# Cross-attention and a ternary feed-forward on one core: heads taken in pairs per batch, keys made on chip, score matmuls as 64-row tiles

## The chip, the cores and the metric

The kernel runs on one core of a Trainium2 chip. The metric is device time in microseconds (us) from the start to the end of one launch; lower is better. Three runs of the kernel before took 846.71, 849.12 and 853.64 us. Durations below come from one further execution that the hardware profiler recorded.

Engines: PE is the matrix engine (PEld its weight loads), DVE the vector engine, ACT the scalar engine, POOL the general engine, SP the engine that issues all the DMAs here. Each works through its own queue in order.

## The reference

`x` is [2, 512, 512] (batch, rows, width), the context `ctx` is [2, 1024, 128]. All of it is fp32.

```python
def layer(x, ctx):
    h = layernorm(x)
    q = (h @ Wq.T).reshape(2, 512, 16, 128)              # 16 heads
    q_big = rope(einsum('bshk,hkq->bshq', q, w_kc_q))    # 384 wide
    q_r = einsum('bshq,hqr->bhsr', q_big, W_qr)          # 64 wide
    kv_r = rope(ctx)                                     # [2, 1024, 128]
    k_r = einsum('bld,hdr->bhlr', kv_r, W_kr)            # 64 wide
    attn = softmax(einsum('bhsr,bhlr->bhsl', q_r, k_r))  # 512 x 1024 per head
    c = einsum('bhsl,bld->bhsd', attn, kv_r)
    x = x + heads(einsum('bhsd,hkd->bhsk', c, w_kc_kv)) @ Wo.T
    y = layernorm(x)                                     # feed-forward:
    return x + bit(silu(bit(y, gate)) * bit(y, val), out)
```

`bit` rounds activations to 8 bits per row and the weights to {-1, 0, 1} times their mean magnitude, then multiplies and adds a bias.

## The kernel before

**Precision.** A value that must be exact to fp32 is held as a high part (`_hi`, fp32r, rounded) and a low part (`_lo`, the rest); a product is three matmuls: high by high, high by low, low by high. The softmax weights are split the same way into two fp16 halves.

**A step** is one head of one batch: 32 steps, in the order of `STEPS`, a table written by hand (twelve heads in pairs, then a special order for the last four). For each step `q_down`, `q_up`, the rotary functions `rot_*` and `q_rank` make the 64-wide query of 512 rows, and `t_hi`, `t_res`, `t_lo` (L613 to L624) arrange it in two tiles `t1`, `t2` of 128 partitions: `t1` holds the high part twice, `t2` holds the low part and the rest.

**Keys.** `key_make` (L870) multiplies `kv_r` by the `W_kr` of two heads, for eight pairs of heads and four blocks of 512 columns: 32 calls of three matmuls, all of them in the first 104 us. `key_hi` and `key_lo` evict the bank. `key_store` (L883) writes both parts to DRAM in two DMAs (60 in all), and `load_keys` (L500) reads them back per step, in two DMAs of 256 KB (60 in all), so that a head's high part lies on partitions 0 to 63 and its low part on 64 to 127. The first two heads get theirs straight from SBUF (`key_direct`, 8 DMAs).

**Scores and softmax.** A step has four *strips* of 128 query rows by 1,024 keys. `score` (L627) makes a strip in four 128-row matmuls, two for each half of the columns:

```python
ps = sc[i, st] = psc.tile([P, L], F32, tag="sc", name=f"sc{i}_{st}")
for n, a in enumerate((t1, t2)):
    for c in range(2):
        nc.tensor.matmul(ps[:, cols], lhsT=a[:, rows], rhs=keys[i][:, cols], start=n == 0, stop=n == 1)
```

A strip then goes through `s_max` (DVE, L638), `s_exp` (ACT, L642, with a read of the sum), `s_scale` and `s_recip` (DVE, 128x1), `e_hi` (ACT, L654), `e_lo` (DVE, L659), and `e_turn` (L665), a transposing DMA that SP issues. `e_lo` is the last that reads the strip's PSUM tile. The pool `psc` has two such tiles, two banks each; the other four banks (`psb`) serve all the other matmuls. The pool `ep` has two tiles for the fp16 weights, which come free when `e_turn` has landed.

**After the softmax** `mix` (L667) multiplies the turned weights by `kv_r`; `c_hi`, `c_lo` evict a step's 512 columns at once; `project` (L684) and `accumulate` (L695) add two heads at a time to `x1`, through `wos[h]`, the product of `w_kc_kv` and `Wo` that `w_out` makes.

**Beside it**, from about 60 us on, the feed-forward weights are read twice: `load_sum`, `w_sum` for their mean magnitude, then `load_tern`, `w_round` (POOL), `w_clip` (DVE), `w_tern` (POOL), `w_store`, in 48 pieces of 512 columns. The feed-forward (`ff_*`) takes the last 100 us.

**The order of issue** is a table, `ISSUE`: for each function a list of places, made by a planner that is not in the file. Calls are sorted by place, and `keep_order` (L411) fixes each engine's order to that. Nothing is reordered at run time; an instruction that waits holds up all behind it on its engine.

Of the kernel before, what the change touches and what calls it, by code (L numbers as in the profile page):

```python
# [1 line left out]

# [23 lines left out]
P = 128  # L26
# [10 lines left out]
STEPS = [(2 * p + n, b) for p in range(6) for b in range(B) for n in range(2)]  # L37
STEPS += [(12, 0), (13, 0), (12, 1), (14, 0), (15, 0), (15, 1), (14, 1), (13, 1)]
NI = len(STEPS)

SPLITS = list(range(H)) + [13]
SPLIT = [h for h, _ in STEPS[:-1]] + [H]

# [3 lines left out]
        760, 701, 693, 742, 895, 812, 888, 941, 1101, 1204, 1135, 1086, 1245, 1192, 1327, 1223, 1507, 1458, 1483,  # L47
        1536, 1600, 1682, 1718, 1649, 1875, 1884, 1925, 1993, 2022, 2044, 2148, 2129, 2303, 2327, 2389, 2521, 2468,
        2532, 2480, 2608, 2674, 2725, 2688, 2809, 2838, 2963, 3027, 2913, 3040, 3110, 3130, 3180, 3396, 3346, 3436,
        3372, 3253, 3243, 3245, 3228, 3474, 3461, 3463, 3458,  # L50
    ),
    "b_hi": (221, 477, 602, 719, 917, 1219, 1350, 1449, 1798, 1974, 2201, 2354, 2578, 2799, 2914, 3124),
    "b_lo": (273, 502, 613, 801, 969, 1290, 1357, 1546, 1802, 1998, 2250, 2375, 2588, 2829, 2979, 3171),
    "c_hi": (
        525, 611, 688, 776, 856, 987, 1043, 1142, 1303, 1368, 1438, 1558, 1668, 1800, 1849, 1990, 2107, 2209, 2285,
        2409, 2536, 2621, 2696, 2803, 2887, 2989, 3075, 3159, 3212, 3292, 3365, 3439,
    ),
    "c_lo": (
        528, 621, 697, 779, 866, 1003, 1053, 1147, 1308, 1375, 1440, 1571, 1670, 1823, 1861, 2004, 2121, 2217, 2291,
        2417, 2549, 2625, 2704, 2804, 2895, 2997, 3084, 3183, 3219, 3300, 3373, 3440,  # L60
    ),
    "e_hi": (
        288, 306, 354, 381, 410, 446, 481, 508, 537, 558, 575, 616, 641, 662, 681, 694, 724, 743, 770, 790, 819, 837,
        854, 881, 901, 925, 943, 972, 989, 1011, 1029, 1059, 1080, 1108, 1129, 1149, 1189, 1212, 1240, 1248, 1291,
        1309, 1337, 1356, 1394, 1417, 1446, 1472, 1502, 1527, 1551, 1579, 1596, 1627, 1647, 1675, 1698, 1722, 1754,
        1777, 1790, 1839, 1844, 1895, 1899, 1937, 1945, 1982, 2007, 2035, 2058, 2088, 2106, 2127, 2158, 2191, 2203,
        2229, 2253, 2275, 2302, 2329, 2353, 2371, 2400, 2423, 2451, 2475, 2510, 2539, 2552, 2577, 2611, 2627, 2657,
        2680, 2697, 2732, 2752, 2773, 2805, 2824, 2847, 2875, 2893, 2909, 2949, 2955, 2987, 2996, 3038, 3023, 3083,
        3092, 3122, 3141, 3160, 3174, 3216, 3234, 3264, 3277, 3316, 3318, 3342, 3354, 3376, 3389,
    ),  # L70
    "e_lo": (
        296, 319, 359, 382, 423, 465, 486, 519, 539, 573, 577, 623, 645, 666, 684, 703, 744, 745, 774, 798, 827, 839,
        863, 885, 911, 927, 946, 973, 1000, 1019, 1041, 1065, 1087, 1117, 1146, 1162, 1194, 1215, 1250, 1258, 1292,
        1324, 1339, 1374, 1408, 1420, 1451, 1481, 1505, 1534, 1557, 1581, 1616, 1630, 1654, 1688, 1704, 1726, 1759,
        1778, 1795, 1846, 1854, 1897, 1907, 1954, 1958, 1986, 2015, 2036, 2068, 2091, 2111, 2133, 2167, 2194, 2214,
        2238, 2267, 2282, 2317, 2332, 2357, 2379, 2402, 2428, 2455, 2484, 2515, 2541, 2569, 2591, 2618, 2635, 2661,
        2683, 2708, 2733, 2757, 2782, 2810, 2827, 2861, 2885, 2901, 2916, 2952, 2957, 2990, 3000, 3041, 3028, 3088,
        3103, 3126, 3145, 3162, 3185, 3221, 3241, 3271, 3281, 3317, 3321, 3352, 3357, 3386, 3393,
    ),
    "e_turn": (  # L80
        309, 366, 403, 414, 453, 497, 518, 523, 545, 599, 607, 638, 648, 683, 707, 729, 766, 771, 791, 813, 831, 857,
        892, 898, 926, 959, 962, 992, 1006, 1046, 1068, 1092, 1095, 1137, 1167, 1179, 1202, 1226, 1267, 1281, 1306,
        1330, 1363, 1385, 1444, 1456, 1465, 1512, 1523, 1548, 1565, 1612, 1629, 1644, 1678, 1711, 1721, 1751, 1766,
        1810, 1814, 1859, 1888, 1909, 1927, 1959, 1972, 2014, 2024, 2063, 2104, 2126, 2152, 2159, 2176, 2215, 2237,
        2256, 2273, 2311, 2351, 2359, 2387, 2401, 2432, 2467, 2476, 2504, 2523, 2568, 2598, 2605, 2649, 2651, 2666,
        2717, 2735, 2768, 2783, 2802, 2812, 2836, 2870, 2888, 2917, 2931, 2967, 2978, 2999, 3020, 3073, 3079, 3101,
        3127, 3144, 3166, 3195, 3201, 3231, 3260, 3286, 3289, 3332, 3334, 3359, 3371, 3404, 3407,
    ),
    "ff_end": (3673, 3641, 3766, 3719, 3813, 3812, 3816, 3821),
    "ff_gate": (  # L90
        3401, 3408, 3424, 3417, 3455, 3482, 3485, 3457, 3525, 3539, 3503, 3497, 3562, 3577, 3548, 3582, 3604, 3625,
        3634, 3611, 3668, 3674, 3652, 3642, 3693, 3725, 3688, 3715, 3754, 3767, 3772, 3745,
    ),
    "ff_hint": (
        3462, 3501, 3490, 3472, 3554, 3570, 3559, 3567, 3608, 3635, 3628, 3614, 3643, 3646, 3665, 3660, 3697, 3722,
        3703, 3709, 3741, 3768, 3747, 3753, 3770, 3782, 3788, 3778, 3801, 3804, 3803, 3802,
    ),
    "ff_hmax": (
        3418, 3435, 3445, 3438, 3469, 3498, 3505, 3489, 3563, 3568, 3593, 3585, 3596, 3620, 3617, 3623, 3645, 3658,
        3654, 3657, 3692, 3696, 3702, 3704, 3729, 3748, 3731, 3749, 3779, 3787, 3791, 3784,  # L100
    ),
    "ff_hround": (
        3451, 3460, 3475, 3450, 3541, 3522, 3553, 3556, 3603, 3615, 3619, 3599, 3631, 3638, 3651, 3653, 3695, 3710,
        3691, 3700, 3728, 3738, 3737, 3736, 3755, 3760, 3761, 3758, 3794, 3796, 3799, 3798,
    ),
    "ff_hscale": (3448, 3518, 3598, 3626, 3679, 3716, 3751, 3793),
    "ff_hturn": (3531, 3590, 3636, 3676, 3733, 3775, 3792, 3807, 3811),
    "ff_in": (
        3392, 3394, 3395, 3400, 3410, 3421, 3405, 3406, 3446, 3449, 3468, 3484, 3479, 3491, 3444, 3447, 3514, 3515,
        3523, 3529, 3496, 3504, 3494, 3502, 3545, 3546, 3564, 3566, 3536, 3537, 3572, 3578, 3583, 3589, 3607, 3616,  # L110
        3618, 3627, 3592, 3594, 3659, 3661, 3663, 3672, 3644, 3648, 3632, 3640, 3685, 3690, 3714, 3718, 3677, 3680,
        3699, 3711, 3744, 3746, 3756, 3763, 3764, 3765, 3724, 3732,
    ),
    "ff_int": (3377, 3398, 3399, 3442, 3573, 3601, 3586, 3705),
    "ff_max": (3362, 3341, 3355, 3339, 3550, 3542, 3551, 3544),
    "ff_norm": (3356, 3326, 3347, 3325, 3535, 3524, 3534, 3530),
    "ff_out": (
        3533, 3547, 3560, 3579, 3595, 3600, 3624, 3629, 3656, 3675, 3723, 3742, 3682, 3708, 3713, 3717, 3743, 3774,
        3781, 3785, 3786, 3790, 3795, 3800, 3805, 3806, 3808, 3809, 3810, 3818, 3819, 3820,
    ),  # L120
    "ff_prod": (
        3416, 3420, 3441, 3429, 3467, 3495, 3500, 3477, 3540, 3555, 3538, 3521, 3575, 3587, 3569, 3602, 3609, 3639,
        3650, 3633, 3683, 3686, 3669, 3666, 3721, 3739, 3706, 3734, 3769, 3783, 3789, 3762,
    ),
    "ff_residual": (3397, 3344, 3415, 3343, 3740, 3797, 3664, 3687),
    "ff_round": (3368, 3391, 3390, 3411, 3565, 3591, 3574, 3597),
    "ff_scales": (3364, 3558),
    "ff_silu": (
        3413, 3414, 3427, 3419, 3464, 3483, 3487, 3471, 3528, 3549, 3519, 3509, 3571, 3580, 3552, 3584, 3606, 3630,
        3647, 3613, 3670, 3684, 3667, 3662, 3701, 3730, 3698, 3720, 3757, 3776, 3780, 3752,  # L130
    ),
    "ff_store": (3727, 3681, 3777, 3735, 3814, 3815, 3817, 3822),
    "ff_turn": (3387, 3432, 3433, 3532, 3581, 3621, 3610, 3707),
    "ff_value": (
        3402, 3409, 3434, 3423, 3453, 3488, 3492, 3452, 3527, 3543, 3516, 3511, 3561, 3576, 3557, 3588, 3605, 3622,
        3637, 3612, 3671, 3678, 3655, 3649, 3694, 3726, 3689, 3712, 3759, 3771, 3773, 3750,
    ),
    "hid_norm": (18, 30, 15, 25, 189, 147, 149, 192),
    "hid_part": (28, 38, 44, 58, 23, 33, 45, 53, 199, 209, 162, 169, 173, 177, 211, 216),
    "hid_turn": (19, 34, 17, 29, 194, 152, 154, 208),  # L140
    "key_direct": (123, 119, 157, 159),
    "key_hi": (
        59, 49, 62, 357, 294, 268, 218, 424, 129, 89, 223, 174, 431, 263, 339, 342, 161, 295, 146, 472, 275, 375, 244,
        459, 187, 180, 467, 251, 330, 361, 207, 387,
    ),
    "key_lo": (
# [278 lines left out]
def cross_attention_ffn(ctx: ExitStack, tc, x, ctxt, wall, wkr, tq, tk, fw, fbias, out):  # L425
# [67 lines left out]
    def key_direct(i, q):  # L493
        if q == 0:
            keys[i] = kst.tile([P, L], F32R, tag="ks", name=f"ks{i}")
# [704 lines left out]
```

## Time and profile before

| | |
|---|---|
| three runs, median (range) | 849.12 us (846.71 to 853.64) |
| the profiled execution, its time | 849.62 us |
| its span, first to last instruction | 847.8 us |
| first score matmul starts | 59.7 us |
| last strip's `s_max` starts | 740.7 us |
| end of the span after it | 107.1 us |
| bytes moved by DMA | 169.93 MB |
| granted clock of PE, mean | 0.955 |

In the page's rows a group is a line of the code on one engine: its count, its busy time in us, the mean duration in ns of one, and the idle time of the engine just ahead of it with what ended that. Two instructions of a group that overlap count once in busy time. The table of slices cuts the span in 40 equal parts; each digit is the busy share of a part in tenths.

### The profile page before, as it was taken

What the parts mean: (1) busy time and instruction counts of PE and PEld (TensorE: products, weight loads), DVE (VectorE), ACT (ScalarE), POOL (GpSimd) and SP (SyncE); (2) the same over time, 40 slices, a digit from 0 to 9 for tenths busy, and PEclk for the clock granted to TensorE, in tenths of its full rate; (3) what the DMA queues carried; (4) which work ended last, traced back from release to release, by engine and by line L of the source; (5) the groups of instructions that cost most, each with busy time, mean ns of one, the idle gap of its engine ahead of it and who ended that gap; (6) DMA issues with size and microseconds to landing.
All of it is one profiled execution on the core that took longest, in us unless ns stands there. A gap on an engine that the chain in (4) does not pass through costs nothing. (4 is left out here: it accounts for less than half of the span.)

```text
span 847.8 us, 12448 instructions
## 1 busy us (share of the span) xinstructions
PE 756.7 (89%) x3914; PEld 548.0 (65%) x3923; DVE 707.6 (83%) x1155; ACT 648.2 (76%) x1090; POOL 589.3 (70%) x529
## 2 busy tenths in 40 slices
PE   6699989989798988678989898898999998899997
PEld 4477756767686766456657676676877776554443
DVE  7899867879778888676879798787999797889995
ACT  4589978889787877666868787677888787859863
POOL 5488876675667777655768788877986694166773
PEclk7699999999999999899989999999999999999999
DMA  9679999998979999986989999979989999954345
GB/s 284 224 255 288 281 224 242 178 211 175 204 165 226 214 238 226 210 183 136 227 194 232 195 198 197 206 157 216 222 159 179 265 173 255 235 107 136 69 99 130
DMA packets 332976, 169.93 MB, mean 200 GB/s; under 512 B 292848, under 2 KB 298992, under 8 KB 332144
## 3 DMA queue, kind: packets, MB, share of 16 engines
q1 hardware_dynamic: 332912, 169.16, 88.5%
q8 instruction: 31, 0.51, 0.2%
q14 instruction: 33, 0.27, 0.1%
HBM read 71.60 MB, written 24.12 MB: 113 GB/s over the span
## 5 line engine op out<-in xcount | busy, mean ns | idle before, releaser
L674 PE MATMUL mps<-et,kvh 128*128 128x256 f16 x1024 | 184.3, 281 | 17.9 <-DMA et<-e 11.8
L659 DVE SCALAR_TENSOR_TENSOR e<-sc,m,e 128x1024 f16<-128x1024 f32 x128 | 163.1, 1279 | 32.2 <-ACT e L654 30.3
L638 DVE TENSOR_REDUCE m<-sc 128x1 f32<-128x1024 f32 x128 | 155.6, 1217 | 32.1 <-PE sc L634 30.6
L654 ACT ACTIVATE e<-sc,m 128x1024 f16<-128x1024 f32 x128 | 142.2, 1114 | 52.2 <-DMA et<-e 39.9
L634 PE MATMUL sc<-ks,t 128*128 128x512 f32 x512 | 148.0, 411 | 21.8 <-DVE e L659 11.9
L642 ACT ACTIVATE sc<-sc,m 128x1024 f32<-128x1024 f32 x128 | 139.5, 1090 | 22.6 <-DVE m L638 22.0
L593 POOL TENSOR_TENSOR c<-c,sinq 128x512 f32<-128x512 f32 x96 | 123.1, 1285 | 44.3 <-ACT c L580 29.6
L604 POOL TENSOR_TENSOR l<-u,h 128x512 fp32r<-128x512 f32 x96 | 123.4, 1290 | 34.5 <-ACT h L600 34.2
L674 PE MATMUL mps<-et,kvl 128*128 128x256 f16 x512 | 143.1, 280 | 0.0
L596 POOL TENSOR_TENSOR u<-u,c 128x512 f32<-128x512 f32 x96 | 124.4, 1299 | 21.2 <-DVE u L590 10.1
L674 PEld LDWEIGHTS <-kvh 128*128 128x128 f16 x1024 | 91.1, 101 | 70.0 <-issue 39.3
L634 PEld LDWEIGHTS sc<-ks,t 128*128 128x128 f32 x512 | 91.4, 191 | 51.0 <-issue 19.9
L590 DVE TENSOR_TENSOR u<-ups,cosq 128x512 f32<-128x512 f32 x96 | 65.2, 682 | 6.9 <-POOL l L604 3.6
L557 PE MATMUL qps<-hidh,whi 128*128 128x512 f32 x128 | 56.6, 443 | 8.8 <-DVE x L697 6.6
L1001 PE MATMUL gv<-ffw,fqt 128*128 128x512 bf16 x250 | 58.8, 379 | 3.7 <-DVE g L1009 2.1
L600 ACT CAST h<-u 128x512 fp32r<-128x512 f32 x96 | 59.0, 618 | 3.0 <-POOL u L596 2.9
L730 POOL TENSOR_SCALAR ft<-ft,fgw 128x512 f32<-128x512 f32 x48 | 33.5, 697 | 38.5 <-DMA ft<-in_fg 14.0
L737 POOL TENSOR_SCALAR fo<-ft 128x512 bf16<-128x512 f32 x48 | 29.7, 618 | 41.9 <-DVE ft L733 24.4
L692 PE MATMUL pps<-woh,ch 128*128 128x512 f32 x128 | 52.5, 410 | 5.7 <-ACT c L580 3.1
L674 PEld LDWEIGHTS <-kvl 128*128 128x128 f16 x512 | 51.4, 100 | 7.0
L557 PE MATMUL qps<-hidl,whi 128*128 128x512 f32 x128 | 53.4, 417 | 0.0
L557 PE MATMUL qps<-hidh,wlo 128*128 128x512 f32 x128 | 52.8, 412 | 0.0
(156 smaller groups left out, 1651.0 us busy)
## 6 DMA issues: line engine op xcount, KB each, us to landing
ks<-kd SPq DMA_DIRECT2D x60, 256.0 KB, 4.6
rawa<-in_wall SPq DMA_DIRECT2D x17, 544.0 KB, 4.8
kd<-kh SPq DMA_DIRECT2D x30, 256.0 KB, 2.9
kd<-kl SPq DMA_DIRECT2D x30, 256.0 KB, 3.2
fd<-fo SPq DMA_DIRECT2D x48, 128.0 KB, 3.0
rawb<-in_wall SPq DMA_DIRECT2D x16, 320.0 KB, 4.3
fs<-in_fg SPq DMA_DIRECT2D x16, 256.0 KB, 3.4
ft<-in_fg SPq DMA_DIRECT2D x16, 256.0 KB, 3.5
```

Of the source, the lines that this page charges most:

```text
L557: nc.tensor.matmul(qs[i][0], lhsT=a[:, c * K:(c + 1) * K], rhs=m[b][:, c, :], start=c == 0 and n == 0, stop=c == 3 and n == 2,)
L590: nc.vector.tensor_tensor(us[i, j], up[i, j], cosq[:, j, :], ALU.mult)
L593: nc.gpsimd.tensor_tensor(cs[i, j], cs[i, j], sinq[:, j, :], ALU.mult)
L596: nc.gpsimd.tensor_tensor(us[i, j], us[i, j], cs.pop((i, j)), ALU.add)
L600: nc.scalar.copy(hs[i, j], us[i, j])
L604: nc.gpsimd.tensor_tensor(ls[i, j], us.pop((i, j)), sb(hs[i, j]), ALU.subtract)
L634: nc.tensor.matmul(ps[:, cols], lhsT=a[:, rows], rhs=keys[i][:, cols], start=n == 0, stop=n == 1)
L638: nc.vector.tensor_reduce(m[:, 0:1], sc[i, st], AX.X, ALU.max, negate=True)
L642: nc.scalar.activation(ps, ps, AF.Exp, bias=m[:, 0:1], accum_out=m[:, 1:2])
L654: nc.scalar.activation(e[:, 0, :], sc[i, st], AF.Copy, scale=sm[i, st][:, 2:3])
L659: nc.vector.scalar_tensor_tensor(e[:, 1, :], sc.pop((i, st)), m[:, 2:3], e[:, 0, :], ALU.mult, ALU.subtract)
L674: nc.tensor.matmul(ps, lhsT=a[:, b, c, :], rhs=et[:, m + c, :], start=c == 0 and n == 0, stop=c == 7 and n == 2)
```

## The change

**Units.** A unit is a pair of heads of one batch, 16 in all, in plain order: `UNITS = [(p, b) for p in range(8) for b in range(B)]`. The special last order and the second read of head 13's weights go.

**Keys when due.** The DRAM copy of the keys is gone, with `key_store`, `load_keys` and `key_direct`: 128 DMAs. The rotated context stays in SBUF (`kth`, `ktl`), `W_kr` comes in eight small loads (`load_wk`), and each unit makes its own keys: two blocks, three matmuls, `key_hi`, `key_lo`, in all as many as before. Head 0 of the pair lies on partitions 0 to 63, head 1 on 64 to 127.

**Scores of two heads.** `t1`, `t2` and the keys hold the two heads of a unit on the two halves of the partitions. `score(u, st)` takes both tiles of `psc` and issues twelve matmuls of 64 rows, alternating between the heads: for each half of the columns high by high, high by low, low by high. `t_hi` becomes one eviction per head instead of two; the rest goes through a scratch tile of the pool `cp`.

**Smaller pieces.** `mix` has a bank per 256 columns, and `c_hi`, `c_lo` run per 256 columns (64 calls of each instead of 32). `wop` has 2 buffers of each kind instead of 4, `lp` 2 instead of 3. In the feed-forward, tiles come from other pools. Each call takes its tile when it runs, and `follow` adds an order (no wait) between users of a tag on different engines.

**A new `ISSUE`.** Every list of places is new. With it, all eight loads of `x` are issued ahead of nearly all the rest, and the first weights of `load_a` come after the tables and most of the context.

The core of the diff:

```diff
+UNITS = [(p, b) for p in range(8) for b in range(B)]
+STEPS = [(2 * p + e, b) for p, b in UNITS for e in range(2)]
...
-    def load_keys(i):
-        h, b = STEPS[i]
-        r = (h % 2) * 64
-        cols = slice(b * L, (b + 1) * L)
-        k = keys[i] = kst.tile([P, L], F32R, tag="ks", name=f"ks{i}")
-        nc.sync.dma_start(sb(k[0:64, :]), kd[h // 2][r:r + 64, 0, cols])
-        nc.sync.dma_start(sb(k[64:128, :]), kd[h // 2][r:r + 64, 1, cols])
+    def load_wk(p):
+        wkp[p] = [const.tile([P, 2 * R], F32, tag="wkr", name=f"wkr{p}")]
+        nc.sync.dma_start(wkp[p][0], wkr[:, p * 2 * R:(p + 1) * 2 * R])
...
+    def t_hi(i):
+        u, e = divmod(i, 2)
+        if u not in ts:
+            ts[u] = [t1p.tile([P, S], F32R, tag="t1", name=f"t1_{u}")]
+        nc.scalar.copy(ts[u][0][half(e), :], rs[i][half(e), :])
+
     def t_res(i):
-        t1, t2 = ts[i]
-        nc.vector.tensor_tensor(t2[64:128, :], rs[i][0:64, :], sb(t1[0:64, :]), ALU.subtract)
+        u, e = divmod(i, 2)
+        td[i] = late["cp"].tile([P, S], F32, tag="c", name=f"d{i}")
+        nc.vector.tensor_tensor(td[i][half(1 - e), :], rs[i][half(e), :], sb(ts[u][0][half(e), :]), ALU.subtract)
...
+    def key_make(u, c):
+        p, b = UNITS[u]
+        kps[u, c] = bank(f"kps{u}_{c}")
+        for n, (a, k) in enumerate(((0, kth), (0, ktl), (1, kth))):
+            nc.tensor.matmul(kps[u, c], lhsT=wkp[p][1][:, a, :], rhs=k[b][:, block(c)], start=n == 0, stop=n == 2)
...
+    def score(u, st):
         rows = slice(st * P, (st + 1) * P)
-        ps = sc[i, st] = psc.tile([P, L], F32, tag="sc", name=f"sc{i}_{st}")
-        for n, a in enumerate((t1, t2)):
-            for c in range(2):
-                cols = slice(c * 512, (c + 1) * 512)
-                nc.tensor.matmul(ps[:, cols], lhsT=a[:, rows], rhs=keys[i][:, cols], start=n == 0, stop=n == 1)
+        ps = [psc.tile([P, L], F32, tag="sc", name=f"sc{2 * u + e}_{st}") for e in range(2)]
+        for e in range(2):
+            sc[2 * u + e, st] = ps[e]
+        for c in range(2):
+            for n, (t, k) in enumerate(((0, 0), (0, 1), (1, 0))):
+                for e in range(2):
+                    nc.tensor.matmul(
+                        ps[e][:, block(c)], lhsT=ts[u][t][half(e), rows], rhs=keys[u, c][k][half(e), :],
+                        start=n == 0, stop=n == 2,
+                    )
...
-    def c_hi(i):
-        cc[STEPS[i]] = [cst.tile([P, S], F32R, tag=t, name=f"{t}{i}") for t in ("ch", "cl")]
-        nc.scalar.copy(cc[STEPS[i]][0], mx[i])
+    def c_hi(i, n2):
+        cc[i, n2] = [cst.tile([P, 256], F32R, tag="ch", name=f"ch{i}_{n2}")]
+        nc.scalar.copy(cc[i, n2][0], mx[i, n2][:, 0:256])
```

The order of `ISSUE` around one group of strips after the change, as the tables give it (unit 12, its second group of rows; each engine's calls in its order):

```
PE    score(12,1)  mix(23,7)  project(11,0)  project(11,2)  project(11,3)  q_rank(26,0..1)  q_down(27,0..2)  q_rank(26,2)  q_down(27,3)  score(12,2)
DVE   c_lo(22,1)  s_max(25,1)  s_max(24,1)  c_lo(23,1)  s_scale, s_recip(25,1)  accumulate(11,0)  s_scale, s_recip(24,1)  accumulate(11,2)  accumulate(11,3)  e_lo(24,1)  wo_lo(12)  e_lo(25,1)
ACT   c_hi(23,1)  s_exp(25,1)  s_exp(24,1)  b_hi(13)  e_hi(24,1)  wo_hi(12)  rot_hi(26,2)  e_hi(25,1)
```

## The prediction

> **What bounds the kernel now.** I read the slices of the page first, then a table of stretches, the groups of the softmax, the waits, and the first microseconds.
>
> ```profile
> PE   6699989989798988678989898898999998899997
> DMA  9679999998979999986989999979989999954345
> ```
>
> Between the start and the feed-forward PE and the DMA engines are both near full.
>
> ```profile
> core 0: us, PE busy (x) PEld busy (x) DVE busy (x) ACT busy (x) POOL busy (x), PEclk, DMA share, GB/s
> 110.00:700.00 590.00, 532.54 (x2878) 405.29 (x2878) 488.47 (x760) 459.08 (x767) 431.63 (x384) 0.97 0.96 202
> 600.00:640.00 40.00, 39.16 (x224) 30.67 (x223) 37.54 (x56) 33.90 (x54) 33.69 (x30) 1.00 0.99 190
> ```
>
> From 110 to 700 us PE is busy 90%, DVE 83%, ACT 78%, POOL 73%, DMA 96%. The third line is a stretch without weight sums to read: PE 98%. So PE is the bound where nothing is late, and elsewhere late transfers cost some.
>
> The pace: the first score starts at 59.7 us, the last strip is made by 740.7, so 16 units (a unit: two heads, one batch, eight strips) take 681 us, P = 42.6 us each, 10.6 for two strips.
>
> ```profile
> L659 DVE SCALAR_TENSOR_TENSOR e<-sc,m,e 128x1024 f16<-128x1024 f32 x128 | 163.1, 1279 | 32.2 <-ACT e L654 30.3
> L638 DVE TENSOR_REDUCE m<-sc 128x1 f32<-128x1024 f32 x128 | 155.6, 1217 | 32.1 <-PE sc L634 30.6
> L654 ACT ACTIVATE e<-sc,m 128x1024 f16<-128x1024 f32 x128 | 142.2, 1114 | 52.2 <-DMA et<-e 39.9
> L634 PE MATMUL sc<-ks,t 128*128 128x512 f32 x512 | 148.0, 411 | 21.8 <-DVE e L659 11.9
> L642 ACT ACTIVATE sc<-sc,m 128x1024 f32<-128x1024 f32 x128 | 139.5, 1090 | 22.6 <-DVE m L638 22.0
> ACT e L654 <- DMA et<-e: 39.9, 27, 3.9
> ```
>
> The loop that matters later: a score tile is free only after its `e_lo` (L659). One strip needs score 1.2 + max 1.2 + exp 1.1 and its sum 0.2 + two 128x1 ops 0.3 + `e_hi` 1.1 + `e_lo` 1.3 + hops, about 6.8 us. With two tiles in turn each tile has 10.6 us per round: 3.8 us of slack for whatever stands ahead in a queue.
>
> **The change, part by part.**
>
> *Row tiles.* The warm-up of before already runs 64-row matmuls on alternating halves:
>
> ```profile
> L455 PE MATMUL warm<-wide x18: 385/390/494, 5.6 to 7.5; 64*128 64x512 f32 x18
> 5.15 0.50 PE L449 MATMUL warm<-ident 128*128 128x128 f32 x3
> 5.58 2.33 PE L455 MATMUL warm<-wide 64*128 64x512 f32 x18
> ```
>
> Eighteen start within 1.95 us; in the trace they start in twos, 4 ns apart, every 0.23 us. That is the pace of single 128-row matmuls (scores start 0.227 apart). So two strips cost 12 / 2 x 0.228 = 1.37 us of PE instead of 8 x 0.228 = 1.82: 0.46 x 64 groups = 29 us less PE. The Trainium skill (TensorEngine Tiling (Array Packing), Key Properties) says that changing the tiling mode drains the array. The row: between the last 128-row matmul and the first 64-row one the start is 0.09 us late, and the first takes 494 ns instead of 390, but a first score after another kind takes 467 too. I take 0.1 us for each of 128 switches, 13 us of PE; by the row alone it could be 0, by a full 390 ns matmul exposed each time, 50. PE keeps 10% of idle time, so it costs little on the path.
>
> *PE in all.* Per unit of after: 24 score slots, 87 others x 0.228 (24 `q_down`, 18 `q_up`, 12 `q_rank`, 24 `project`, 6 keys, 3 `w_out`), 96 mix x 0.109: 5.5 + 19.8 + 10.5 = 35.8 us. The keys (96 matmuls, 22 us) only move, from the first 104 us into the units.
>
> *DMA.* Gone: 60 stores and 60 loads of 256 KB and 8 of 128 KB.
>
> ```profile
> ks<-kd SPq DMA_DIRECT2D x60, 256.0 KB, 4.6
> kd<-kh SPq DMA_DIRECT2D x30, 256.0 KB, 2.9
> kd<-kl SPq DMA_DIRECT2D x30, 256.0 KB, 3.2
> et<-e SPq DMA_TRANSPOSE x128, 5.0
> ```
>
> In the packet records 2,048 B take 106 ns and 4,096 B 253: (8,192 x 0.106 + 3,840 x 0.253) / 16 = 115 us of the 16 engines, of 750 (88.5% of the span). SP also loses 128 issues of 0.46 us. A transposing DMA keeps 2,048 packets of 24 ns, 3.1 us of all engines; per unit DMA falls to about 34 us. What this can give back is the waits on late transfers: ACT 39.9 us on turned weights, POOL 33 on weight pieces. They are hidden in part, and where they matter they are in P.
>
> *ACT, DVE, POOL.* `t_hi` falls by 32 x 0.58 = -18.5 us on ACT. `c_hi` and `c_lo` in halves: between rows of 192 and 512 elements a 256-wide piece is about 0.40 us, so 64 x 0.40 - 32 x 0.59 = +7 on ACT, +5 on DVE. Keys: 1.2 and 1.4 us more per unit on ACT and DVE instead of at the start. DVE per unit is then about 36.6 us, ACT 33, POOL unchanged (rotary 3.87 us a piece).
>
> *The wait that is added.* `score` now takes both tiles, and its matmuls alternate, so it starts when the later `e_lo` of the group before is done, and no strip is made meanwhile. The shortest round: both strips ready at 1.64; max 1.65 to 2.88 and to 4.06 (DVE); exp with sum 2.93 to 4.1 and to 5.3 (ACT); `e_hi` to 6.3 and 7.4; `e_lo` 6.4 to 7.65 and to 8.85; next score at 9.1. In that round DVE has 5.6 us for the two strips and must fit 3.5 to 4 us of other work into the gaps. The Trainium skill (TensorEngine Tiling (Array Packing), PSUM Bottleneck) says that tiling speeds up TensorE but not the emptying of PSUM. The rows agree in size: 0.46 us saved on PE against 2 x (2.5 DVE + 2.4 ACT) of emptying that is unchanged and no longer overlaps the next score. By PE alone the sum would be 849 - 29 = 820; by the emptying it is what follows.
>
> I followed the order of issue of three units by hand with the durations above, as if no DMA or POOL were ever late. Rounds: unit 3: 9.6, 9.7, 10.1, 11.8 = 41.2. Unit 7: 9.0, 10.0, 10.2, 12.2 = 41.4. Unit 12: 9.5, 12.6, 9.9, 11.9 = 43.9. The 12.6 is the one shown in the section on the change: `accumulate` of three `project` calls stands on DVE ahead of `e_lo(24,1)`; they wait for PE, which waits for `c_lo(23,1)` at 4.4; projects end at 6.0, 7.4, 8.8; so `e_lo` runs 9.5 to 10.75, `wo_lo` to 11.4, the second `e_lo` to 12.65. Queued behind on PE is the score, and with it every later matmul. The last round of a unit is long since `t_lo` of the next unit follows the last `e_lo`. Mean 42.2.
>
> *Late turns.* The two `e_turn` now leave together: issue takes SP 3.1 us (median), landing 5.0 after issue. The second `e_lo` ends at 8.85, its turn is issued at 10.8, lands at 15.8; in the next round its tile is wanted at 9.1 + 6.3 = 15.4 (tightest) to 16.9. A quarter of landings took over 5.9. I take 0.25 us a round, 1.0 a unit; bounds 0 and 3. P = 43.2.
>
> *At nothing:* `wop` with two buffers, `lp` with two, the other tiles of the feed-forward, `follow`. `w_out` must now wait for the last `project` of the unit before; PE's idle tenth and three other kinds of matmul cover that, and without them it costs at most a `project`, 1.4 us a unit, 22 in all. The feed-forward's end stays bound by its 83 us of matmuls.
>
> *Start.* The first score needs two heads, not one: three more pieces of 3.87 us on POOL, 11.6 in all, against keys no longer made for other pairs. POOL was idle 22 of the first 60 us. Bounds 59.7 and 71.3; I take 65. *End.* 107.1 us follow the last strip, on PE for 83 of feed-forward; nothing there is removed. I take 107, within 4.
>
> Sum: 65 + 16 x 43.2 + 107 = 863 us of span, against 847.8. The profiled run took 849.62, 1.8 over its span, and 0.5 over the median: 864 us.
>
> **The rivals.** *Faster:* the DMAs were what held the units back. For: DMA share 0.96; where no sums are read the pace was 36 to 38 us; PE and DMA both shed work. Then the unit runs at P = 40.5, near the tight rounds: 65 + 648 + 107 + 1.3 = 821. It decides below P = 41.7. Against: three units by hand, none under 41.2. *No change:* as by hand, nothing late: P = 42.2 gives 848. *Slower still:* the rounds meet POOL and PE late as well, P = 45.5: 901. *The tiles do not run side by side:* a round grows by 1.37 us, 88 in all: 952; the warm-up speaks against it.
>
> **How the numbers follow.** Forecast (P about 43.2) 0.42; faster 0.22; no change 0.18; slower still 0.15; tiles in turn 0.03. About 1% is what a measurement of this kernel can tell from no change. Faster 0.22, same 0.18, slower 0.42 + 0.15 + 0.03 = 0.60. The range, 830 to 900, runs from P = 41 to 45.4 and leaves out a tenth on each side; the forecast's own is 852 to 878.
>
> **What would show it.** Right: 64 groups of scores with DVE idle before `s_max` waiting for PE, and PE idle before the score waiting for `e_lo`, far above 11.9 us; rounds of 10 to 11 us; score matmuls in twos 4 ns apart; DMA share near 0.8. Wrong: PE above 90% between 110 and 700 us, or P below 41.7. The start is wrong if the first score is before 60 or after 71.

## The result, and the profile after

The changed kernel takes 889.86 us (median of four runs, 888.65 to 892.57), the kernel before 849.59 beside it (846.71 to 853.64). The ratio is 1.0475, 95% interval 1.0425 to 1.0525: slower by nearly 5%, where 864 us, 1.7% slower, was forecast. The profiled execution took 889.37 us, its span is 887.6.

By the three terms of the forecast's sum:

| us | before | forecast | after |
|---|---|---|---|
| first score starts | 59.7 | 65 | 72.8 |
| 16 units, up to the last `s_max` | 681.0 (42.56 each) | 691 (43.2) | 685.4 (42.84) |
| span after it | 107.1 | 107 | 129.4 |
| span | 847.8 | 863 | 887.6 |

The loop came out near the forecast, even a little quicker. The 24 us that are missing lie at its two ends. First the slices of the page after, then the table of stretches:

```profile
PE   5577898999989999999999989999998777867877
PEclk8787999999999999999999999999999887989999
DMA  9313667888887998899986877878678774523135
```

```profile
core 0: us, PE busy (x) PEld busy (x) DVE busy (x) ACT busy (x) POOL busy (x), PEclk, DMA share, GB/s
110.00:700.00 590.00, 554.82 (x3216) 409.63 (x3214) 518.75 (x820) 462.32 (x802) 445.67 (x401) 1.00 0.81 173
600.00:640.00 40.00, 37.05 (x220) 27.08 (x220) 34.91 (x56) 31.40 (x52) 32.91 (x31) 1.00 0.73 157
```

The DMA engines fell from 96% to 81% between 110 and 700 us. VectorE rose from 83% to 88%, PE from 90% to 94%. In the slices PE stands at 5 to 7 for the first 90 us, and at 6 to 8 for the last 130, with the granted clock below full in both.

The groups of the softmax and the score, each with all that ended its idle time:

```profile
L681 DVE SCALAR_TENSOR_TENSOR e<-sc,m,e 128x1024 f16<-128x1024 f32 x128 | 161.3, 1279 | 24.6 <-ACT e L676 22.8
L660 DVE TENSOR_REDUCE m<-sc 128x1 f32<-128x1024 f32 x128 | 151.4, 1215 | 17.9 <-PE sc L653 17.2
L676 ACT ACTIVATE e<-sc,m 128x1024 f16<-128x1024 f32 x128 | 140.0, 1117 | 16.5 <-ACT sc L664 7.0 <-DMA et<-e 3.3 <-issue 3.0
L664 ACT ACTIVATE sc<-sc,m 128x1024 f32<-128x1024 f32 x128 | 139.3, 1089 | 27.1 <-DVE m L660 26.8
L653 PE MATMUL sc<-kh,t 64*128 64x512 f32 x512 | 125.1, 430 | 17.1 <-DVE e L681 13.7 <-DVE t L620 2.3 <-ACT t L609 0.5
```

`e_hi` waited 39.9 us for turned weights before; now 3.3. The other waits of the softmax did not take its place, in sum they fell: `s_exp` waits for the maximum 22.0 us before and 26.8 now, `e_lo` for `e_hi` 30.3 and 22.8, `s_max` for the score 30.6 and 17.2. Durations are unchanged. What grew is the work per unit: VectorE is busy 35.2 us of each before (488.47 / 590 x 42.56) and 36.8 now (518.75 / 590 x 41.9, the pace of the first 14 units).

Unit by unit the first scores start at 72.8, 114.5, 156.7 and so on: the first 14 units take 41.9 us each, from 40.4 to 43.8. Then unit 14 (counted from 0) takes 48.5 and the last one 50.2 to its last `s_max`. The last unit starts at 708.0; in the kernel before, the last eight strips start at 705.0. From there the old kernel needs 142.8 us to the end, the new one 179.6. So 37 of the 40 us are lost behind that point. Those stretches, before and then after (the last eight strips, up to the last `accumulate`, the rest; a packet is counted where it starts, so the DMA share of a short stretch can pass 1):

```profile
705.00:741.00 36.00, 29.75 (x162) 21.63 (x160) 27.49 (x55) 27.96 (x48) 8.26 (x9) 0.91 1.07 237
741.00:767.00 26.00, 24.27 (x131) 15.11 (x132) 23.46 (x41) 16.88 (x28) 16.66 (x19) 1.00 0.46 94
767.00:848.00 81.00, 72.24 (x322) 31.60 (x327) 68.76 (x146) 55.92 (x90) 47.14 (x47) 1.00 0.47 114
```

```profile
708.00:758.00 50.00, 37.20 (x187) 25.39 (x188) 30.44 (x59) 33.09 (x54) 5.72 (x7) 0.80 0.65 145
758.00:775.00 17.00, 13.96 (x81) 8.88 (x82) 9.10 (x16) 9.50 (x15) 3.31 (x5) 0.90 0.40 68
775.00:888.00 113.00, 83.97 (x351) 35.41 (x356) 78.28 (x164) 63.02 (x99) 55.67 (x55) 0.95 0.35 85
```

In the first stretch no engine is busy more than three quarters of the time. In the second the old kernel runs the feed-forward of batch 0 beside the last projects (PE 24.3 of 26 us, POOL 16.7); the new one hardly does (POOL 3.3 of 17), and so has 113 us left instead of 81. Batch 0 itself is ready later: its last `accumulate`, before and then after, ends at 708.4 and 728.6 us.

```profile
707.69 0.68 DVE L697 TENSOR_TENSOR x<-pps,x 128x512 f32<-128x512 f32 x1
```

```profile
727.23 1.38 DVE L719 TENSOR_TENSOR x<-pps,x 128x512 f32<-128x512 f32 x2
```

### The profile page after: what moved, and what is told of

Read it like the earlier page. It is cut to its first block, busy times and chain, and to the rows that moved or that the text cites. A ratio compares the mean times of both kernels' runs of the same rounds, so it can differ in the third digit from the quotient of the medians.

```text
span 887.6 us, 12735 instructions
## 1 busy us (share of the span) xinstructions
PE 773.0 (87%) x4169; PEld 538.8 (61%) x4179; DVE 718.8 (81%) x1187; ACT 638.3 (72%) x1097; POOL 585.0 (66%) x532
## 3 DMA queue, kind: packets, MB, share of 16 engines
q1 hardware_dynamic: 319696, 136.09, 69.6%
## 5 line engine op out<-in xcount | busy, mean ns | idle before, releaser
L696 PE MATMUL mps<-et,kvh 128*128 128x256 f16 x1024 | 176.3, 277 | 9.7 <-DMA et<-e 4.0
L681 DVE SCALAR_TENSOR_TENSOR e<-sc,m,e 128x1024 f16<-128x1024 f32 x128 | 161.3, 1279 | 24.6 <-ACT e L676 22.8
L660 DVE TENSOR_REDUCE m<-sc 128x1 f32<-128x1024 f32 x128 | 151.4, 1215 | 17.9 <-PE sc L653 17.2
L664 ACT ACTIVATE sc<-sc,m 128x1024 f32<-128x1024 f32 x128 | 139.3, 1089 | 27.1 <-DVE m L660 26.8
L653 PE MATMUL sc<-kh,t 64*128 64x512 f32 x512 | 125.1, 430 | 17.1 <-DVE e L681 13.7
L696 PEld LDWEIGHTS <-kvh 128*128 128x128 f16 x1024 | 95.8, 99 | 44.2 <-issue 23.5
L653 PEld LDWEIGHTS sc<-kh,t 64*128 64x128 f32 x512 | 71.1, 189 | 54.5 <-issue 33.2
L991 PE MATMUL gv<-ffw,fqt 128*128 128x512 bf16 x249 | 65.7, 411 | 30.7 <-DVE g L999 19.6
L572 ACT COPY c<-ups 128x512 f32<-128x512 f32 x64 | 37.5, 588 | 59.6 <-PE ups L568 33.5
L653 PE MATMUL sc<-kl,t 64*128 64x512 f32 x256 | 72.2, 415 | 0.0
L991 PEld LDWEIGHTS <-fqt 128*128 128x128 bf16 x256 | 26.2, 103 | 68.5 <-issue 36.4
L1013 POOL TENSOR_TENSOR hd<-g,v 128x512 f32<-128x512 f32 x31 | 39.2, 1272 | 42.3 <-DVE v L1007 15.2
```

Of the source, the lines that this page charges most:

```text
L653: nc.tensor.matmul(ps[e][:, block(c)], lhsT=ts[u][t][half(e), rows], rhs=keys[u, c][k][half(e), :], start=n == 0, stop=n == 2,)
L660: nc.vector.tensor_reduce(m[:, 0:1], sc[i, st], AX.X, ALU.max, negate=True)
L664: nc.scalar.activation(ps, ps, AF.Exp, bias=m[:, 0:1], accum_out=m[:, 1:2])
L681: nc.vector.scalar_tensor_tensor(e[:, 1, :], sc.pop((i, st)), m[:, 2:3], e[:, 0, :], ALU.mult, ALU.subtract)
L696: nc.tensor.matmul(ps, lhsT=a[:, b, c, :], rhs=et[:, m + c, :], start=c == 0 and n == 0, stop=c == 7 and n == 2)
L991: nc.tensor.matmul(gps[t, j][:, n * 512:(n + 1) * 512], lhsT=fqt[t][:, c, :], rhs=w[c // 2][:, c % 2, block(j)], start=c == 0, stop=c == 3,)
```

## Experiments

Kernels with a_ are the changed one with an edit, those with b_ the kernel before with one. The kernel before was run beside each group: 846.7, 846.5, 845.8 and 850.7 us.

**The transfers: b_nokeys and a_dma.** The first takes the traffic of the keys from the old kernel:

```diff
     def load_keys(i):
-        (two DMAs of 256 KB into keys[i])
+        keys[i] = keys[i - 2]
     def key_store(p, q):
-        (two DMAs of 256 KB)
+        pass
```

> The kernel before without the traffic of the keys: nothing is stored to DRAM and nothing is read back, every step uses the keys of the first two (it leaves out 120 DMAs of 256 KB; the rest of the work and the order of issue are as before). Theory 'swap of bounds' (the old units were held by the DMA engines, the new ones by the chain through the paired score tiles, and the two cost about the same): the old order, free of that traffic, runs its units at 37 to 40 us instead of 42.6: 770 to 810 us. Rival 'hidden anyway' (the old units were held by their own order and PE, not by transfers): 835 to 847 us.

808.28 us (802.55 to 810.55), ratio 0.952 (0.945 to 0.959); 40.1 us a unit, start and end as before (59.2 and 106.5). Its slices and stretches:

```profile
PE   7599999999899989678999999899999998898997
DMA  9523669797869999876989988699878899745445
```

```profile
110.00:700.00 590.00, 552.30 (x3037) 422.89 (x3037) 515.22 (x814) 486.88 (x814) 442.77 (x393) 0.98 0.88 188
600.00:640.00 40.00, 39.73 (x231) 30.76 (x230) 35.17 (x54) 31.73 (x50) 25.80 (x23) 1.00 0.87 197
```

So 38 us of the old kernel were these transfers, their issues on SP included. Freed of them it has PE busy 99% of the second stretch. The time is near the upper end of what was expected, the pace at it. The second experiment puts transfers back into the new kernel, four before each block of keys:

```diff
     def key_make(u, c):
+        for n in range(4):
+            d = dram.tile([P, 512], F32, name=f"d{u}_{c}_{n}")
+            nc.sync.dma_start(d, wall[4 * c + n, :, 0:512])
```

> The changed kernel with transfers put back: each unit also copies eight blocks of 256 KB of the weights to unused DRAM, 128 DMAs, about as many issues and bytes as the keys took before; nothing waits for them. If the relief of the DMA engines is worth nothing here (waits on transfers were hidden): within 4 us of 889.9. If the relief gave the units time that the coupling then took away: +15 to +40 us, 905 to 930, with late turns again in front of e_hi (39.9 us before, 3.3 now).

965.69 us: 76 more, above both ranges, 47.7 us a unit. `e_hi` waits for turned weights again, and VectorE behind it:

```profile
DVE e L447 <- ACT e L442: 45.1, 41, 4.4
ACT e L442 <- DMA et<-e: 34.6, 19, 4.3
```

They put back 123 us of the 16 engines' time (76.9% of 963.2 less 69.6% of 887.6). These copies go from DRAM to DRAM, so their price is not that of the keys. But the relief is real in the new kernel; it is not why it is slow.

**PE: a_unpair.** The two heads' matmuls in another order:

```diff
-        for c in range(2):
-            for n, (t, k) in enumerate(((0, 0), (0, 1), (1, 0))):
-                for e in range(2):
+        for e in range(2):
+            for c in range(2):
+                for n, (t, k) in enumerate(((0, 0), (0, 1), (1, 0))):
```

> The changed kernel with the twelve score matmuls of a group in another order: six of head 0, then six of head 1, so that no two run side by side and head 0 no longer waits for head 1's tile. If single 64-row matmuls take 0.228 us each, a group costs 2.74 us of PE instead of 1.37: 88 us in all. If PE sets the pace of the units: +60 to +90 us, 950 to 980. If the coupling of the two tiles sets it (head 0 starts up to 1.3 us sooner, head 1 is the later by no more than before): -15 to +25 us, 875 to 915.

893.42 us (893.18 to 895.98), 3.5 more; 43.0 us a unit. PE doesn't set the pace, though it is busy nearly all the time. One thing in the expectation was wrong: a group doesn't cost 2.74 us. In the trace head 1's first three matmuls start beside head 0's last three, and from the first start to the last end the twelve take 2.24 us in the median, against 1.65 at best and 1.98 in the median for the alternating order. The alternation thus saves a quarter to half a microsecond of PE a group, some 20 us in all, and 3.5 us of time. The two groups of its scores and its stretch:

```profile
L416 PE MATMUL sc<-kh,t 64*128 64x512 f32 x512 | 144.8, 425 | 7.1 <-DVE e L444 7.1
L416 PE MATMUL sc<-kl,t 64*128 64x512 f32 x256 | 87.2, 400 | 1.0 <-DVE kl L405 0.9
```

```profile
110.00:700.00 590.00, 570.34 (x3193) 432.36 (x3192) 514.28 (x815) 456.46 (x794) 439.84 (x396) 1.00 0.80 172
```

PE does more and waits less for emptied tiles (7.1 us instead of 13.7): the extra work fills time in which it had waited. The edit also lets head 0 start without head 1's tile, and the run does not separate that gain from the cost of the extra work.

**VectorE: a_dve and b_dve.** The same edit in both kernels:

```diff
-        nc.vector.tensor_tensor(qs[i][2], qs[i][0], sb(qs[i][1]), ALU.subtract)
+        for _ in range(3):
+            nc.vector.tensor_tensor(qs[i][2], qs[i][0], sb(qs[i][1]), ALU.subtract)
```

> The changed kernel with more VectorE work: each q_lo runs three times with the same result, four further evictions of 128x512 a unit, by the 0.68 us of one 2.7 us a unit and 43 in all. If VectorE and the chain through it set the pace of the new units: most of it is paid, +25 to +45 us, 915 to 935. If PE or the transfers set it: 0 to +10 us.

> The kernel before with the same further VectorE work, 2.7 us a unit, 43 us in all. If its units were held by transfers, with VectorE 83% busy: 0 to +20 us on 846 to 849. If by VectorE: +35 to +45 us.

The new kernel pays 34 of the 43 us (923.87 against 889.86), the old one 14 (860.63 against 846.50). Both as the first theory of each expected. By the profiled executions the 2.7 us of each unit cost 2.2 in the new kernel (45.05 instead of 42.84, in an execution of 931 us, the slowest of the four) and 0.3 in the old (42.89 instead of 42.56). The new units hang on VectorE and what is chained to it, the old ones hardly. In the same stretch VectorE is busy 89% in the new and 87% in the old, so the busy share alone would not have told this:

```profile
110.00:700.00 590.00, 540.82 (x3048) 394.31 (x3047) 525.34 (x837) 442.36 (x770) 425.03 (x382) 0.98 0.77 163
```

```profile
110.00:700.00 590.00, 529.42 (x2852) 395.57 (x2851) 515.59 (x804) 456.76 (x761) 429.33 (x380) 0.98 0.95 201
```

**Paired tiles in the old order: b_nokeys_pair and b_pair.** In the old kernel's table of places every even strip's `score`, `s_max` and `s_exp` move to right before the odd strip's. Other places move with them, which the expectation does not say: of the even strips nearly all `s_scale` and `s_recip`, 53 of 64 `e_hi`, 30 `e_lo` and 4 `e_turn`, most of them to places right behind the moved `s_exp`.

```diff
     "score": (
     ...
-        231, 236, 301, 333,
+        235.5, 236, 332.5, 333,
     ...
     "s_max": (
     ...
-        233, 239, 314, 338,
+        238.5, 239, 337.5, 338,
     ...
     "e_hi": (
     ...
-        288, 306, 354, 381,
+        288, 306, 361.8, 381,
     ...
```

> The kernel before without the traffic of the keys (as in the run without it: every step uses the first two keys, 120 DMAs left out), and with its strips paired as in the change: the score, s_max and s_exp of each even strip are issued right before those of the odd one, so both tiles must be empty before either is filled again. Nothing else moves. Theory 'coupling' (the chain through two paired tiles sets the new pace): most of the 38 us that the missing traffic gave is lost again, units near 42 to 44 us instead of 40.1: 835 to 870 us. Rival (the pairing is harmless, the new units are slow for other reasons): within 8 us of 808.

> The kernel before, all its transfers kept, with its strips paired in the same way. If the coupling costs by itself what the transfers cost, and the two hide each other in part: +10 to +40 us on 847, 857 to 887. If the strips had slack enough: within 5 us.

951.11 and 959.23 us: 143 more than without the pairing in the one, 113 in the other, 49.0 and 49.4 us a unit; far above both expected ranges. So the pairing, put into an order that is not planned for it, costs far more than the new kernel shows, whose units take 42 us in a table of their own. And in this order the same missing transfers are worth 8 us instead of 38. The stretch of b_pair and its `e_lo` and `s_max`:

```profile
110.00:700.00 590.00, 470.46 (x2370) 353.18 (x2370) 407.97 (x636) 388.99 (x656) 365.20 (x327) 0.92 0.79 173
```

```profile
L409 DVE SCALAR_TENSOR_TENSOR e<-sc,m,e 128x1024 f16<-128x1024 f32 x128 | 163.8, 1282 | 90.4 <-ACT e L404 89.8
L388 DVE TENSOR_REDUCE m<-sc 128x1 f32<-128x1024 f32 x128 | 150.6, 1217 | 36.4 <-PE sc L384 35.9
```

VectorE stands 89.8 us before `e_lo` for `e_hi`, against 30.3 in the old order and 22.8 in the new kernel. But 61 of the 90 us lie ahead of the even strips' `e_lo`, most of them in pieces of 1.23 us, about one `e_hi`: the moved steps of an even strip follow each other directly, so VectorE stands through the whole `e_hi`. No engine is over 80%, and the DMA engines fall to 79% by themselves. So these two runs say what this order costs, not what the pairing costs in the changed kernel.

So why the new units, freed of the transfers, take 41.9 us and not the 40.1 of b_nokeys is not shown. Besides the pairing there is a plainer reason: VectorE is busy 36.8 us a unit instead of 35.0 there (515.22 / 590 x 40.11), since the evictions of the keys now lie in the units, and a_dve shows that such work is paid for. A changed kernel with its two heads' strips staggered was not tried.

**The start: a_start, a_start2, a_rot, a_start3.** The first gives the first loads the old order, with batch 1's layer norm at the places 128 to 165:

```diff
-    "load_x": (0, 7, 12, 6, 3, 1, 8, 4),
+    "load_x": (0, 3, 4, 1, 82, 77, 119, 85),
-    "load_ctx": (21, 38, 41, 68),
+    "load_ctx": (7, 16, 27, 38),
-    "ln_rstd": (22, 58, 3252, 3400),
+    "ln_rstd": (22, 128.24, 3252, 3400),
     ...
```

> The changed kernel with the first loads in the old kernel's order: x of batch 0, its context and the first weights first, x of batch 1 and its layer norm later. Theory 'ends' (the units cost what they cost before, the loss of 40 us is the first 73 us and all that follows unit 14): the first q_down starts near 25 us instead of 31.3, the first score near 66 instead of 72.8, all later times move with it: 880 to 885 us against 889.9. Rival 'two heads' (the start is late only because two heads' queries must be made): first score stays at 71 to 74, time within 2 us of 889.9.

899.72 us, the wrong way. The first `q_down` came at 24.2 us, as meant, but VectorE then stood 6.4 and 3.5 us before the late layer norm, PE 12.8 behind it, and the first score came at 84.1. The second spreads that layer norm:

```diff
-    "ln_sqrt": (20, 128.22, 3250, 3398),
+    "ln_sqrt": (20, 150.5, 3250, 3398),
-    "ln_rstd": (22, 128.24, 3252, 3400),
+    "ln_rstd": (22, 151.5, 3252, 3400),
     ...
```

> The changed kernel with the first loads in the old order as in the run before, but with the layer norm of batch 1 spread over ScalarE's idle stretches so that VectorE doesn't stand before it (there it stood 6.2 and 3.5 us, and PE 12.8). The first q_down starts near 25 us as there. If what is left of the late start is the load order: first score at 65 to 68 instead of 72.8, 882 to 886 us. If it is the second head and the first query of the next unit, which lie ahead of the first score on PE and POOL: first score at 71 to 74, within 3 us of 889.9.

895.30 us, and the first score at 75.8 with a first `q_down` at 23.9:

```profile
23.91 0.80 PE L312 MATMUL qps<-hidh,whi 128*128 128x512 f32 x1 [4.26 <-POOL whi L259]
```

Seven microseconds won at the first query were all lost before the first score, so an earlier query alone does not bring an earlier score. The third moves work from POOL:

```diff
-        nc.gpsimd.tensor_tensor(ls[i, j], us.pop((i, j)), sb(hs[i, j]), ALU.subtract)
+        (nc.vector if i < 2 else nc.gpsimd).tensor_tensor(ls[i, j], us.pop((i, j)), sb(hs[i, j]), ALU.subtract)
```

> The changed kernel with the six rot_lo of the first unit's two heads on VectorE instead of POOL (6 x 1.28 us). If POOL's rotary work for two heads sets the first score (it is busy nearly all the time from 42 to 71 us): first score at 66 to 70 instead of 72.8, 882 to 887 us. If PE or the loads set it: within 2 us of 889.9.

888.16 us (886.26 to 888.64), first score at 72.1. That is nothing: in four other edits that leave the start as it is (a_pool, a_unpair, a_dma, a_tail) it comes between 70.9 and 73.0. So these 7.7 us of POOL are not what is waited for. The last takes the next unit's first query out of the way:

```diff
     "q_down": (
     ...
-        179, 195, 196, 198,
+        231.01, 231.03, 231.05, 231.07,
     ...
     "q_hi": (
     ...
-        199,
+        234.09,
     ...
```

> The changed kernel with the loads of a_start2 and, beyond that, the first query of unit 1 (q_down, q_up and the rotary functions of step 2) issued after the first score instead of ahead of it. If the late start is depth (work of the next unit stands in the in-order queues ahead of the first score): first score at 65 to 70 instead of 75.8 there and 72.8 in the changed kernel, 884 to 888 us. If it is only the second head of the first unit: first score within 2 us of 73 to 76.

899.69 us, first score at 76.1, and the first round 16 us long instead of 10.9. In this run POOL stands 10.0 us in one piece for a rotary input, behind batch 1's turns on PE. Each edit uncovered another wait; none moved the first score ahead of 72. That two heads must be made first is consistent with all four, and the changed kernel's trace agrees: the query of head 1 is what comes last ahead of the first group, whose matmul for head 1 waits for that head's `t_hi`:

```profile
72.94 0.58 ACT L609 CAST t<-rps 64x512 fp32r<-64x512 f32 x1
73.57 0.50 PE L653 MATMUL sc<-kh,t 64*128 64x512 f32 x1 [0.26 <-ACT t L609]
```

But no run shows it alone: the cause of the late start stays open.

**The end: a_pool and a_tail.** The products of the feed-forward start late on POOL. Before, and then after (start, length, instruction, idle time ahead):

```profile
749.44 1.27 POOL L1022 TENSOR_TENSOR hd<-g,v 128x512 f32<-128x512 f32 x1 [0.20 <-ACT g L1012]
750.97 1.27 POOL L1022 TENSOR_TENSOR hd<-g,v 128x512 f32<-128x512 f32 x1 [0.26 <-ACT g L1012]
```

```profile
766.33 0.62 POOL L974 TENSOR_SCALAR fq<-fy 128x512 bf16<-128x512 f32 x1 [7.68 <-ACT fy L970]
772.82 0.62 POOL L974 TENSOR_SCALAR fq<-fy 128x512 bf16<-128x512 f32 x1 [5.86 <-ACT fy L970]
773.59 2.52 POOL L1013 TENSOR_TENSOR hd<-g,v 128x512 f32<-128x512 f32 x2
```

Two reasons were possible: the tiles, held until the last project, or the queues, in which `ff_int` of rows 3 and 1 stands ahead and waits for ScalarE, which is busy with the last strips.

```diff
-        n, tag = ((wop, "woh"), (wop, "wol"), (kst, "kh"), (kst, "kl"))[j]
+        n, tag = ((wspl, "wlo"), (const, "bl" if t % 2 else "bh"), (kst, "kh"), (kst, "kl"))[j]
```

> The changed kernel with one edit: the products hd of the feed-forward take tiles that are free early (low weights, bh, bl) for j = 0 and 1 instead of those of the output weights, which are held until the last project. The order of issue is untouched. Rival 'pools' (the feed-forward of batch 0 stands still because its tiles are held until the last project at 774 us): the first product starts near 753 instead of 773.6 and the end comes 8 to 20 us sooner, 870 to 882. Theory 'order' (the queues are in the wrong order, the tile is not what is waited for): within 2 us of 889.9.

889.98 us, the first product at 772.5: nothing. The tiles are not it. For a_tail the 554 calls from the last unit's first score on were placed anew, by a list schedule over their dependences and the durations of the trace, with the longest remaining chain first.

```diff
-    "ff_max": (3265, 3266, 3267, 3268, 3416, 3449, 3450, 3451),
+    "ff_max": (3308, 3297, 3301, 3321, 3397, 3401, 3404, 3407),
-    "ff_int": (3274, 3350, 3382, 3341, 3467, 3527, 3569, 3587),
+    "ff_int": (3330, 3332, 3338, 3350, 3423, 3425, 3445, 3453),
     "s_max": (
     ...
-        3188, 3225, 3272, 3298, 3199, 3228, 3261, 3308,
+        3196, 3233, 3259, 3294, 3192, 3235, 3262, 3302,
     ...
```

> The changed kernel with another order of issue from the last unit's first score (708 us) to the end: the last unit's softmax, turns and projects stand ahead of batch 0's layer norm and feed-forward wherever both are due; tiles and work are the same. Theory 'order of the end' (the last strips waited for feed-forward work in the queues, and the feed-forward for the last projects): the last max starts at 742 to 748 instead of 758, the end 5 to 15 us sooner, 875 to 885. Rival 'depth' (a whole unit of eight strips is left when the last query is made, whatever the order): within 4 us of 889.9, with batch 0's feed-forward later by what the strips are sooner.

878.96 us (876.73 to 880.94), ratio 1.039 (1.035 to 1.043) against 1.0475: 10 us less of span. The last `s_max` starts at 750.1 instead of 758.2, a little later than expected, and the feed-forward of batch 0 at 767.9 instead of 747.9; once started, its sixteen groups take 44 us instead of 68 (before: 42). Its stretches, cut as above:

```profile
705.00:750.00 45.00, 34.59 (x179) 24.39 (x179) 27.68 (x51) 26.48 (x47) 4.53 (x6) 0.81 0.83 182
750.00:773.00 23.00, 13.83 (x74) 9.60 (x75) 10.80 (x23) 13.38 (x22) 6.64 (x8) 0.78 0.60 134
773.00:877.00 104.00, 86.92 (x367) 37.10 (x372) 81.14 (x166) 62.21 (x98) 54.27 (x53) 0.95 0.31 66
```

Both theories hold in part. From the last unit's first score to the end it takes 172.3 us, where the changed kernel takes 179.6 and the old one 142.8: order gives 7 us of the 37 here (the other 3 us of the 10 lie ahead of the edit), and 11 in a_all against a_start3 (171.5 and 182.5). In the first two stretches, though, PE still idles 23% and 40% of the time, VectorE and ScalarE 38% to 53%. The depth shows in the count of strips: when the last rotary piece is done (717.0 us before, 707.0 after), six strips are left in the old kernel and eight in the new, and the last of them begins its `s_max` 24 us later in the old and 51 in the new. Seen from the end of batch 0's last `accumulate` (708.4 before, 728.6 after, 731.1 in a_tail), 139.4, 159.0 and 146.4 us follow. So the better order takes back 13 of the 20 us lost behind that point, and nothing of the 20 by which batch 0 is ready later.

**All repairs: a_all.**

The edits of a_tail, a_start3 and a_rot together:

> The changed kernel with all three repairs together: this start, the first unit's rot_lo on VectorE, and the order of the end that took it from 889.9 to 879.0. If the repairs add up: 868 to 877 us, still 2.5% or more above the kernel before, since the units keep 42 us; what is left then is the depth of a pipeline of pairs at both ends and no gain in between.

885.05 us, ratio 1.042 (1.038 to 1.046), no better than a_tail alone (1.035 to 1.043): the start of a_start3 is no repair, it costs about what the new end gives (first score at 74.5, first unit 46.0 us). No version here beats the kernel before.

## Why the prediction was wrong, step by step

**What bounds the old kernel: right as far as tested.** PE and the transfers were both named. b_nokeys shows what the second are worth (38 us). That PE is the next bound is only read from its 99% in one stretch; no run added PE work to the old kernel.

**The transfers: right in size.** 115 us of the 16 engines were forecast to go; 88.5% of 847.8 less 69.6% of 887.6 is 132, and the share is 0.81 where 0.8 was said. The rival *faster* went one step too far with it: the first 14 units came to 41.9 us, not 40.5. Whether the pairing takes the rest or VectorE's added work is open, as said above.

**PE: right that it is not the bound, wrong in its mark.** I held PE above 90% to disprove the forecast; it came out at 94%, and it disproves nothing, since 20 us more of PE work cost 3.5. The sum of slots, 35.8 us a unit, was set against the busy time of the page, which counts more: by the same slots the old unit is 36.2 us, where 532.54 / 590 x 42.56 = 38.4 is shown. Row tiles were sized from the warm-up's pace, 1.37 us a group. Counted alike (to the last start, plus one slot) the best group takes 1.49 and the median 1.82, no less than eight single slots. In 31 of the 64 groups head 1's first matmul starts over 0.3 us after head 0's, mostly because its tile waits for `e_lo`, and head 0's second matmul follows right behind it. Even so the score matmuls keep PE busy 128.9 us in the run, overlaps counted once, against 148.0 before: 19 less, where 29 less 13 were forecast.

**The added wait: right in place, other in look.** The shortest rounds measure 8.2 to 9.3 us, 9.1 was worked out. By hand and in the trace: unit 3 41.2 and 42.6, unit 7 41.4 and 40.7, unit 12 43.9 and 41.3; the 12.6 us round that was forecast there took 10.9. The mean of 42.2 without late turns stands against 41.9 for the first 14 units. But the wait does not show between score and `s_max` (30.6 us before, 17.2 after) or between `e_lo` and score (11.9 and 13.7), where I told the reader to look, and the waits of VectorE and ScalarE for each other did not grow in sum either. So the pace is right, but that the added wait makes it is not shown. VectorE's work per unit is right too (36.6 us worked out, 36.8 measured), and a_dve shows that the new units hang on it. The rule of the Trainium skill that tiling does not speed up the emptying of PSUM (TensorEngine Tiling (Array Packing), PSUM Bottleneck) is borne out here: a strip's `s_max` and `e_lo` take 1,217 and 1,279 ns before, 1,215 and 1,279 after. And undoing the side-by-side order costs 3.5 us, four further evictions a unit cost 34.

**Late turns: wrong.** I added 1.0 us a unit for them. `e_hi` waited 3.3 us for turns in the whole run. By luck this term hid 16 us of the miss: with P at 42.2, as worked by hand, the sum would have been 847, not 863. In the loop's total it stands against 14.9 us more in the last two units, which the prediction had not priced.

**The start: too small.** 65 was taken between 59.7 and 71.3, and 72.8 came. The bound was built on 11.6 us of POOL's rotary work; a_rot takes 7.7 of them from POOL and gains nothing.

**The end: this step failed.** "I take 107, within 4", since nothing in the feed-forward was removed. It took 129.4, and the two units ahead of it, which I had priced like all others, 6.6 and 8.3 us more than the first fourteen. (Unit 14 takes 46.4 to 49.1 us in every edited kernel; no run was made for it.) The feed-forward's matmuls are the same; what went, by the stretches above, is its cover. The old table of steps ended in a special order, three heads of batch 1 behind the last of batch 0; it is named among the changes, and the prediction gives it no price. In plain order two heads are left, both in one unit, whose eight strips come after the last query with little beside them. Of the 37 us behind the last unit's start, a_tail and a_all show 7 to 11 to lie in the order of the queues. How the other 26 to 30 divide between the depth of the pair, batch 0's later end and the lower clock, no run tells: an old kernel with plain steps, or the new with the special ones, was not tried. So the step that failed is known, and most of its cause is argued from the traces.

In sum 7.8 us at the start, 22.4 at the end, and 16 x 0.36 = 5.8 back from the loop: 24.4, from 863.2 to 887.6.

## What to carry to other kernels

When a change makes the unit of a pipeline larger, price its filling and its draining apart from its pace: read what runs beside the last unit in the profile before, and ask what will still run there. Before counting what the transfers and other engines save, count what the change adds to the engine on which the new units will hang. And a full engine is not yet the bound; only work added to it shows that.

## What the runs showed of the hardware

- Row tiles overlap without being interleaved: six matmuls on one half of the rows and then six on the other took 2.24 us from the first start to the last end (median of a_unpair), where twelve in turn would take 11 slots of 0.228 and one length of 0.39, 2.90. The second half's first three start beside the first half's last three (in one group 0, 333, 562, 795, 1031 and 1255 ns for the one, 569, 903 and 1139 ns for the other's first).
- The granted clock of PE was below full in stretches in which PE had much idle time, but it does not follow the busy share: 0.80 from 708 to 758 us with PE busy 74%, and 0.95 from 775 to 888 us, also at 74%; 1.00 from 110 to 700 at 94%; in b_pair, with PE at 80%, 0.92 over the same 590 us.
